# A GRU over 128 steps on one Trainium2 core: x loaded once into a ring of four tiles, and half of each crossing copied by ScalarE

## The chip, the cores and the metric

The kernel runs on one core of a Trainium2 chip. The core has a matrix engine (PE in the profile; PEld is its loading of weights, which overlaps with its products), a vector engine (DVE), a scalar engine (ACT), a general engine (POOL), a sync engine (SP) that here only issues DMAs, and 16 DMA engines. The engines run side by side, each through its own list of instructions in the order written, and they wait for each other by semaphores. The metric is the time of the whole program on the device in microseconds (us); lower is better. A change is called faster or slower here if it is more than 0.5%, about 6 us, away.

## The reference

64 sequences of 128 steps and 512 features go through a gated recurrent unit (GRU) with 512 hidden values, everything in float32. After every fourth step, except the last of all, the state also goes through a product with Wp and a tanh before the next step uses it. The output is x plus the states.

```python
def step(h, inp):
    x_t, prop = inp                          # prop: (t+1) % 4 == 0 and t < 127
    comb = jnp.concatenate([x_t, h], axis=-1)
    z = jax.nn.sigmoid(comb @ Wz + bz)
    r = jax.nn.sigmoid(comb @ Wr + br)
    comb2 = jnp.concatenate([x_t, r * h], axis=-1)
    h_cand = jnp.tanh(comb2 @ Wh + bh)
    h_new = (1.0 - z) * h + z * h_cand
    h_next = jnp.where(prop, jnp.tanh(h_new @ Wp + bp), h_new)
    return (h_next, h_new)                   # scan over T = 128; out = x + all h_new
```

## The kernel before, in words

**Two kinds of work.** The products with the state, h @ W, depend on the step before and form the recurrent chain. The products with x don't, and are made ahead of it as filler: PE runs them while the chain is on the other engines. The 128 steps are 32 groups of four. From group 2 on, two groups (a "duo", 15 of them) are handled together by a scheme of the Strassen and Winograd kind that saves multiplications: a duo has seven `Batch` objects, each of seven sub-products, and each sub-product is a few units of eight matmul instructions in the trace (L695, tiles `x` in PSUM). ACT and DVE bring the sub-products out of PSUM (L725 to L739) into four SBUF tiles `mb`, POOL adds them up there (L303, `mb<-mb,mb`), and the four results of a group are its crossings.

**A crossing.** `send` (L783) takes one result from its `mb` tile to the tile `gx` of a pair of steps. The result is four blocks of 64 partitions by 384 floats: block (h, d) lies on the partitions of half h and belongs on those of half d. All four go by DMA, issued by SP (L789). There are 124 crossings. A step reads its `gx` tile in its gate sums (L1142 and others) and as the start values of its candidate (L987).

**The step.** A step of the chain has seven blocks of 16 matmuls for the gates R and Z (L275; left operands `ht`, results in `bank_A`, `bank_B`, `bank_C`, `bank_E`), two sigmoids on ACT for each half of the batch (L1011), and two candidate products of 32 matmuls (`wc`), each with a tanh on ACT (L1230). From the new state, DVE makes the left operands of the next step: it transposes (L271), ACT copies one piece into PSUM (`first_copy`, L961), and DVE takes sums and differences of the pieces (L968 to L970). The block `bank_E<-wrz` (S1) needs L969, which needs L961. Every fourth step has two more products of 32 (`wp`) and two more tanhs (L1261). The last four steps are computed plainly, with the weights of h unsummed: since the summing overwrote part of Wr and Wz, four pieces of these, 256 KB each, are loaded again (tiles `raw`, L1032).

**What sets the order.** All of it is a list written at build time by a planner in Python. It keeps its own estimates: `clock` (PE's time by fixed costs), `pool_free` and `sync_free`. `fill(n)` puts up to n units of filler at one of the places of a step (`PLACES` and, for steps 0 to 3, `HEAD`). It takes a unit only if its operands are there by the estimates, and it takes a sub-product that writes a new `mb` tile only if the tile's former results have all been sent (`room`, set by `over`). `flush` puts the ACT or DVE evictions behind a sub-product, `drip` issues up to two DMAs per place, a crossing whose sum is done by the estimate or else another DMA, and `have_sums` forces the DMAs of a crossing that a step needs at once. Since the estimates decide which unit stands where, another estimate moves units.

**x.** x is loaded twice. Once into `xr`, a ring of two group tiles in which POOL adds the states to x (L303, `xr<-xr,h`) and from which the result is stored (L1073); and once into `xs` (two tiles, L129), from which DVE makes the transposed x for the filler (`join_x`, L344). At the end the `xs` tiles take the weights `raw`.

Of the kernel before, what the change touches and what calls it, by code (L numbers as in the profile page):

```python
# [9 lines left out]
F32 = mybir.dt.float32  # L10
# [8 lines left out]
def kernel(  # L19
# [14 lines left out]
    nc = tc.nc  # L34
# [17 lines left out]
    const = ctx.enter_context(tc.tile_pool(name="const", bufs=1))  # L52
    one = ctx.enter_context(tc.tile_pool(name="one", bufs=1))
    two = ctx.enter_context(tc.tile_pool(name="two", bufs=2))
    ps_c = ctx.enter_context(tc.tile_pool(name="ps_c", bufs=1, space=PSUM))
    ctx.enter_context(tc.manual_schedule())

# [85 lines left out]
            )  # L143

    both_queues = (nc.sync, nc.scalar)
    xr, xs = {}, {}
# [21 lines left out]
    def landing(name):  # L168
        did.add(name)
        lands[name] = max(sync_free, clock) + 3500  # L170

    def load_xs(g, later=None):
        if g < GROUPS:
            xs[g] = one.tile([P, Q4, S, J], F32, tag=f"xs{g % 2}", name=f"xs_{g}")
            load_x(xs[g], g * Q4, Q4, later)
            if later is None:
                did.add(("xs", g))
            else:
                last = later.pop()
                later.append(lambda: (last(), landing(("xs", g))))  # L180

    new_xr(0)
    x_rows = one.tile([P, Q4, S, J], F32, tag="xs0", name="x_rows")[:B].rearrange(
        "b t h u -> b (t h u)"
    )
    for t in range(2):
        both_queues[t].dma_start(out=x_rows[:, ts(t, D)], in_=x[:, t, :])
    for k0, k1 in ((0, 1), (1, 2), (2, K)):
# [17 lines left out]
    def later_loads():  # L206
        load_w(wrz[:, :, R], Wr[D:])
        load_w(wrz[:, :, Z], Wz[D:])
        load_step(3)
        new_xr(1)  # L210
        load_x(xr[1], Q4, Q4)
        load_w(wc, Wh[D:])
        load_x(xr[0], 0, 2)
        load_xs(2)
        load_w(wp, Wp)
        for q in range(NQ):
            nc.sync.dma_start(
                out=bias_p[part(q)],
                in_=bp.rearrange("(o j) -> o j", o=1)[:, ts(q, J)].broadcast_to([V, J]),
            )  # L220
# [87 lines left out]
            nc.gpsimd.tensor_sub(o, a, b)  # L308
            Gp.busy(o)

    crossing, plain_dmas = [], []

    def issue(run):
        nonlocal sync_free
        run()
        sync_free = max(sync_free, clock) + 690

    def cross():
        ready, run, then = crossing.pop(0)
        issue(run)  # L320
        then()

    def drip(n):
        for _ in range(n):
            if sync_free > clock + 1400:
                return
            if crossing and crossing[0][0] <= clock + 300:
                cross()
            elif plain_dmas:
                issue(plain_dmas.pop(0))  # L330
            else:
                return

# [448 lines left out]

    def send(q, n, g, i):  # L783
        new_gx(q)
        parts = [(h, d) for h in range(S) for d in range(2)]
        for k, (h, d) in enumerate(parts):

            def run(h=h, d=d):
                nc.sync.dma_start(  # L789
                    out=gx[q][ts(d, 2 * V), h, n].rearrange("p b g u -> p (b g u)"),  # L790
                    in_=M[g, i][ts(h, 2 * V), d].rearrange("p b g u -> p (b g u)"),
                )

            def then(k=k):
                if k == len(parts) - 1:
                    sent.add((q, n))
                    over(g, i, sync_free + 2700)

            crossing.append((pool_free, run, then))

    todo = []
    steps_done = -1
# [18 lines left out]
    def join_next():  # L821
        for n, (g, i, after) in enumerate(joins):
            if all(a in did for a in after) and (
                g is None or g < FIRST or ("xs", g) in did and lands.get(("xs", g), 0) <= clock
            ):
# [7 lines left out]
                if i == Q4 - 1 and g >= FIRST:  # L833
                    load_xs(g + 2, plain_dmas)
                if i == Q4 - 1 and g == GROUPS - 1:
                    load_raw()
                poll()
                return True
        return False
# [140 lines left out]

    def have_sums(t):
        while t >= Q4 and not all((t // 2, n) in sent for n in range(C)):
            cross()

    def seed_h(t, lane, h):
        have_sums(t)
# [35 lines left out]
            )  # L1022

    hT = ht.rearrange("p n v -> p (n v)")
    raw_late = []

    def load_raw():
        for k in range(2):
            raw_late.append(one.tile([P, 2, H], F32, tag=f"xs{k}", name=f"raw_{k}"))
            for i in (R, Z):  # L1030
                plain_dmas.append(
                    lambda k=k, i=i: nc.sync.dma_start(  # L1032
                        out=raw_late[k][:, i],
                        in_=gates_in[i][D:].rearrange("(p k) n -> p k n", k=K)[:, k],
                    )
                )

    def gate_product(t, lane, i):
        for k in range(K):
# [29 lines left out]
    def store(g, n):  # L1069
        for h in range(S):  # L1070
            for q in range(NQ):
                plain_dmas.append(
                    lambda h=h, q=q: nc.sync.dma_start(  # L1073
                        out=out[ts(h, V), g * Q4 : g * Q4 + n, ts(q, J)],
                        in_=xr[g][part(q), :n, h, :],
                    )
                )

    def behind(t, h_new):
        nonlocal steps_done  # L1080
        g, j = divmod(t, Q4)
        steps_done = t
        unsaved.append((t, h_new))
        poll()
        if t == T - 2:
            save()
            store(g, Q4 - 1)
            while crossing or plain_dmas:
                cross() if crossing else issue(plain_dmas.pop(0))
        elif j == 0 and g > 0:  # L1090
            store(g - 1, Q4)
        if j == 1 and g >= 1 and g + 1 < GROUPS:
            load_x(lambda: new_xr(g + 1), (g + 1) * Q4, Q4, plain_dmas)
            last = plain_dmas.pop()
            plain_dmas.append(lambda: (last(), did.add(("xr", g + 1))))

    unsaved = []

    def save():
        while unsaved:  # L1100
            t, h_new = unsaved.pop()
            g, j = divmod(t, Q4)
            while g >= FIRST and ("xr", g) not in did:
                issue(plain_dmas.pop(0))
            o = xr[g][:, j].rearrange("p h (e k) -> p h e k", k=K)
            Gp.tensor_add(o, o, h_new.rearrange("p h (k e) -> p h e k", k=K))

    def step(t, h_old, v_1):
# [27 lines left out]
        else:  # L1136
            have_sums(t)
            fill(next(places), eager)
            flush(at_act, 300)
            first_copy()  # L1140
            block(u_ps, A11, raw(0, 0), start=True)
            nc.vector.tensor_add(row[0][:, :J], u_ps, rz_in(t, 0, 0))  # L1142
# [1 line left out]
            save()  # L1144
            fill(next(places), eager)
            flush(at_act, 300)
            block(row[0][:, :J], A12, raw(1, 0))
            block(e_ps, S1, raw(0, 1), start=True)
            flush(at_dve, 0, 1 if t > 3 else 9) or join_next()
# [5 lines left out]
            flush(at_dve, 900, 1 if t > 3 else 9) or join_next()  # L1155
            fill(next(places), eager)
            flush(at_act, 300)
            block(u_ps, S3, summed(3))
            nc.vector.tensor_add(  # L1159
                row[1][:, : 2 * J].rearrange("p (n j) -> p n j", n=2),  # L1160
# [123 lines left out]

    def late_step(t, gate_r, gate_z):
        flush(at_act, 300)
        flush(at_dve, 300)
# [86 lines left out]
    )  # L1374
    for d in range(DUOS):
        add_duo(d)

    for _ in range(2):
        join_next()
    h, v_1 = h_init, None  # L1380
    for t in range(T):
        if t == 1:
            load_xs(3, plain_dmas)
        h, v_1 = step(t, h, v_1)


# [37 lines left out]
```

## Time and profile before

| | |
|---|---|
| time, median of 3 runs | 1266.87 us (1265.43, 1266.87, 1271.63) |
| profiled execution | 1270.18 us; from its first to its last instruction 1268.3 us |
| granted TensorE clock in it | 0.996 |
| busy share of the span | PE 97%, PEld 89%, DVE 71%, ACT 45%, POOL 72% |
| bytes moved by DMA | 112.43 MB, 106.68 MB of them on the queue of SP's and ACT's DMAs |

In the views, a line such as "L695 PE MATMUL x<-sums_w,s ... x8" is a group of 8 instructions of program line 695 that write the tile `x` and read `sums_w` and `s`. In the timeline, the first number is the start in the span, the second the time to the end of the group, and in brackets behind it stands how long the engine idled before it and what ended that ("<-issue": nothing that the profile shows). In the list of waits, the three numbers are us in total, how often, and the longest. The groups overlap, because the engines are pipelined: the time that a group really costs its engine is the distance to the start of the next one.

### The profile page before, as it was taken

Reading aid. Unit: us, or ns where it says so; the run is one execution under the profiler, and the core shown is the slowest. Engines: PE = TensorE matmul, PEld = TensorE weight load, DVE = VectorE, ACT = ScalarE, POOL = GpSimd, SP = SyncE. Lnnn points to the kernel's source line nnn. Section 1 sums busy time; section 2 is a strip of 40 time slices with the busy share of each in tenths; the row PEclk is TensorE's granted clock in tenths of the full one; section 3 lists DMA queues with packets and bytes.
Section 4 is the critical chain, followed back from the end, with each engine's and each line's share of the span. In section 5 each row is a group of like instructions: output and inputs, shape, how many; then the busy total and the mean of one; then the engine's idle time right before and its main releaser. Section 6 shows DMA issues by size and latency. Waiting matters only on the chain.

```text
span 1268.3 us, 85362 instructions
## 1 busy us (share of the span) xinstructions
PE 1233.8 (97%) x37576; PEld 1131.0 (89%) x37576; DVE 900.8 (71%) x2964; ACT 565.1 (45%) x1838; POOL 916.6 (72%) x1045
## 2 busy tenths in 40 slices
PE   7899999999999999999999999999999999999997
PEld 6798999999998999989899999988889999999887
DVE  5656777777776777777777777777777777777665
ACT  1344444444444444444444444444444444444443
POOL 1796787876868778687786868778677786868751
PEclk9999999999999999999999999999999999999999
DMA  7323333333343332333324343332333324333322
GB/s 243 87 51 79 89 92 86 83 92 87 74 102 84 85 90 74 92 96 83 83 71 101 82 102 82 90 89 72 91 82 83 97 73 99 85 90 93 86 61 62
DMA packets 153090, 112.43 MB, mean 89 GB/s; under 512 B 20836, under 2 KB 148976, under 8 KB 152720
## 3 DMA queue, kind: packets, MB, share of 16 engines
q1 hardware_dynamic: 152288, 106.68, 33.2%
q8 instruction: 295, 4.83, 1.7%
q14 instruction: 75, 0.61, 0.2%
q0 software_dynamic: 256, 0.14, 0.0%
q10 hardware_dynamic: 176, 0.16, 0.0%
HBM read 41.36 MB, written 16.78 MB: 46 GB/s over the span
## 4 chain that ended last, share of the span: by engine, by line
PE 95%; issue 2%; DVE 1%; ACT 1%; POOL 1%; DMA 0%; DVEq 0%; POOLq 0%; ACTq 0%
PE x L695 39%; PE bank_B L275 20%; PE bank_C L275 15%; PE bank_A L275 13%; PE bank_E L275 5%; PE x L275 2%; DMA stage<-in_L_cond_bh_dram 0%; POOL wx L308 0%; ACT bank_A L1011 0%; DVE xT L344 0%; DVE h L1234 0%; DVE bank_E L1233 0%; DVE rh L1119 0%; DVE ht L271 0%; POOL stage L191 0%
## 5 line engine op out<-in xcount | busy, mean ns | idle before, releaser
L303 POOL TENSOR_TENSOR mb<-mb,mb 128x768 f32<-128x768 f32 x167 | 304.6, 1832 | 172.5 <-ACT mb L739 82.1
L695 PE MATMUL x<-sums_w,s 128*32 128x192 f32 x2880 | 184.9, 326 | 0.0
L303 POOL TENSOR_TENSOR xr<-xr,h 128x256 f32<-128x256 f32 x127 | 111.3, 876 | 94.8 <-DVE h L1234 94.7
L275 PE MATMUL bank_B<-wrz,ht 128*32 128x128 f32 x4000 | 173.7, 273 | 4.9 <-issue 2.9
L275 PE MATMUL bank_A<-tr,ht 128*32 128x128 f32 x3936 | 168.9, 273 | 1.4 <-issue 0.8
L275 PEld LDWEIGHTS bank_B<-wrz,ht 128*32 128x32 f32 x4000 | 133.0, 110 | 13.4 <-issue 8.8
L275 PE MATMUL bank_B<-wc,rhT 128*32 128x128 f32 x4096 | 142.1, 274 | 2.9 <-DVE rhT L271 0.5
L275 PE MATMUL bank_C<-wc,rhT 128*32 128x128 f32 x4096 | 141.2, 273 | 0.0
L275 PEld LDWEIGHTS bank_A<-tr,ht 128*32 128x32 f32 x3936 | 129.5, 110 | 8.4 <-DVE bank_B L1153 4.2
L275 PEld LDWEIGHTS bank_B<-wc,rhT 128*32 128x32 f32 x4096 | 112.8, 109 | 24.2 <-ACT bank_A L1011 16.0
L695 PE MATMUL x<-sums_w,o 128*32 128x192 f32 x1920 | 124.9, 326 | 1.0 <-issue 1.0
L275 PEld LDWEIGHTS bank_C<-wc,rhT 128*32 128x32 f32 x4096 | 119.8, 110 | 0.5 <-ACT bank_C L1125 0.2
L695 PEld LDWEIGHTS x<-sums_w,s 128*32 128x32 f32 x2880 | 111.3, 110 | 4.9
L1159 DVE TENSOR_TENSOR bank_C<-bank_A,gx 128x256 f32<-128x256 f32 x123 | 53.2, 433 | 82.1 <-PE bank_A L275 82.1
L1011 ACT ACTIVATE bank_A<-bank_B 128x128 f32<-128x128 f32 x123 | 32.2, 262 | 154.6 <-DVE bank_C L1159 151.2
L1119 DVE TENSOR_TENSOR rh<-bank_A,h 128x128 f32<-128x128 f32 x192 | 56.1, 292 | 52.7 <-ACT bank_A L1011 46.2
L725 ACT COPY x<-x 128x384 f32<-128x384 f32 x108 | 50.3, 465 | 86.9 <-PE x L695 86.9
L303 POOL TENSOR_TENSOR mb<-mb 128x768 f32<-128x768 f32 x47 | 86.2, 1834 | 2.5
L731 ACT COPY u<-x 128x384 f32<-128x384 f32 x108 | 51.8, 479 | 78.1 <-PE x L695 78.1
L739 ACT COPY mb<-x 128x384 f32<-128x384 f32 x108 | 52.1, 482 | 77.1 <-PE x L695 73.9
L271 DVE STREAM_TRANSPOSE rhT<-rh 128x128 f32<-128x128 f32 x256 | 79.8, 312 | 9.0
L275 PE MATMUL bank_E<-wrz,ht 128*32 128x128 f32 x1968 | 85.0, 274 | 0.2 <-issue 0.2
(884 smaller groups left out, 3085.6 us busy)
## 6 DMA issues: line engine op xcount, KB each, us to landing
gx<-mb SPq DMA_DIRECT2D x496, 96.0 KB, 2.5
xr<-in_x_dram SPq DMA_DIRECT2D x248, 64.0 KB, 2.8
out_dram<-xr SPq DMA_DIRECT2D x248, 64.0 KB, 2.6
xs<-in_x_dram SPq DMA_DIRECT2D x240, 64.0 KB, 2.9
wx<-in_L_cond_Wz_dram SPq DMA_DIRECT2D x2, 512.0 KB, 6.2
wx<-in_L_cond_Wh_dram SPq DMA_DIRECT2D x2, 512.0 KB, 8.0
wrz<-in_L_cond_Wr_dram SPq DMA_DIRECT2D x2, 512.0 KB, 9.3
wrz<-in_L_cond_Wz_dram SPq DMA_DIRECT2D x2, 512.0 KB, 10.8
```

The source lines that it names most:

```text
L271: nc.vector.transpose(out=dst, in_=src)
L275: nc.tensor.matmul(region[part(q)], lhsT=left, rhs=rhs(q), start=start, stop=True, skip_group_check=True,)
L303: nc.gpsimd.tensor_add(o, a, b)
L695: nc.tensor.matmul(v[part(2 * h + c)], lhsT=left[:, ts(h, V)], rhs=right[:, c::2], start=j in (1, 5) and m == 0 and n == 0, stop=True, ski ...
L725: nc.scalar.copy(self.a, self.u)
L731: nc.scalar.copy(self.u_sb, self.u)
L739: nc.scalar.copy(self.block(1, 0), runs(self.u))
L1011: nc.scalar.activation(gate_out(dst), gate_in(lane, i), AF.Sigmoid)
L1119: nc.vector.tensor_mul(rh[:, h], r_ps[:, h], h_old[:, h])
L1159: nc.vector.tensor_add(row[1][:, : 2 * J].rearrange("p (n j) -> p n j", n=2), bcast(u_ps), G[t][:, 1, :, :2].rearrange("p n g u -> p n (g ...
```

## The change

x is loaded once, into a ring of four tiles `xr`, which serves both the transposes and the output. The tile of group g+3 takes the place of the tile of group g-1; its load is queued behind that group's store, and the planner holds it back until it reckons the store to be done. Of each crossing, the two blocks with h = d are copied by ACT (`staying`, placed by `stay` at three places of a step, after `flush(at_act)`, at most one at each; two in a late step), and the two others go by DMA as before. A tile `mb` counts as free 1000 ns after the copy by the planner's clock, and as before 2700 ns after the last DMA is issued. `have_sums` forces copies as well as DMAs. The weights `raw` now go into `wx`, the weights of x, after the last batch has read it.

```diff
-            xr[g] = two.tile([P, Q4, S, J], F32, tag="xr", name=f"xr_{g}")
+            xr[g] = ring.tile([P, Q4, S, J], F32, tag="xr", name=f"xr_{g}")
...
-    def load_xs(g, later=None):
...
+    def load_group(g):
+        def when():
+            return stored.get(g - 4, 0)
+
+        held_back = []
+        load_x(lambda: new_xr(g), g * Q4, Q4, held_back)
+        last = held_back.pop()
+        held_back.append(lambda: (last(), landing(("x", g))))
+        for run in held_back:
+            plain_dmas.append((when, run))
...
+    def stay(late=200, most=1):
+        while most and staying and staying[0][0] <= clock + late:
+            staying.pop(0)[1]()
+            most -= 1
...
-        src = xr[g] if g < FIRST else xs[g]
+        src = xr[g]
...
-        parts = [(h, d) for h in range(S) for d in range(2)]
-        for k, (h, d) in enumerate(parts):
-
-            def run(h=h, d=d):
-                nc.sync.dma_start(
-                    out=gx[q][ts(d, 2 * V), h, n].rearrange("p b g u -> p (b g u)"),
-                    in_=M[g, i][ts(h, 2 * V), d].rearrange("p b g u -> p (b g u)"),
-                )
...
-                    over(g, i, sync_free + 2700)
+        for h in range(S):
+
+            def run(h=h):
+                nc.sync.dma_start(out=to(h, 1 - h), in_=of(h, 1 - h))
+
+            crossing.append((ready, run, lambda: one_done(sync_free + 2700)))
+            staying.append(
+                (ready, lambda h=h: (nc.scalar.copy(to(h, h), of(h, h)), one_done(clock + 1000)))
+            )
...
         while t >= Q4 and not all((t // 2, n) in sent for n in range(C)):
-            cross()
+            if staying and (not crossing or staying[0][0] <= crossing[0][0]):
+                staying.pop(0)[1]()
+            else:
+                cross()
...
-    raw_late = []
+    raw_late = [wx[:, k, :2] for k in range(2)]
...
             fill(next(places), eager)
             flush(at_act, 300)
+            stay()
             first_copy()
...
+    task("raw", load_raw, ("b", DUOS - 1, 6))
```

On PE, the order differs from step 6 on for a few steps. Before, the candidate products of step 5 (`wc`) and the blocks A11, A12 and S1 of step 6 stand without filler between them:

```order
L275 MATMUL bank_B<-wc,rhT_1818 32x128 x16
L275 MATMUL bank_C<-wc,rhT_1818 32x128 x16
L275 MATMUL bank_A<-wrz,ht 32x128 x8
L275 MATMUL bank_B<-wrz,ht 32x128 x8
L275 MATMUL bank_E<-wrz,ht 32x128 x8
L275 MATMUL bank_A<-tr_86,ht 32x128 x8
L695 MATMUL x_101<-wx,o_2_1428 32x192 x4
```

Of the change, at the same place (its line 279 is line 275 before, 704 is 695):

```order
L279 MATMUL bank_B<-wc,rhT_1803 32x128 x16
L279 MATMUL bank_C<-wc,rhT_1803 32x128 x16
L704 MATMUL x_104<-wx,o_2_1421 32x192 x4
L704 MATMUL x_104<-sums_w,o_2_1421 32x192 x4
L704 MATMUL x_103<-sums_w,s_2_1424 32x192 x8
L279 MATMUL bank_A<-wrz,ht 32x128 x8
L704 MATMUL x_105<-wx,s_2_1424 32x192 x4
L704 MATMUL x_105<-sums_w,s_2_1424 32x192 x4
L704 MATMUL x_102<-sums_w,xT_973 32x192 x4
L279 MATMUL bank_B<-wrz,ht 32x128 x8
L279 MATMUL bank_E<-wrz,ht 32x128 x8
L279 MATMUL bank_A<-tr_89,ht 32x128 x8
```

Four units of filler now stand ahead of A11 and three between A11 and A12 (a unit is x4 here, and eight instructions in the trace); at step 7 it is alike. After step 9 or so, PE's order is the same as before up to the last steps' names.

On ACT, the copies stand between the other work. Before, around `first_copy` (L961) and the gates (L1011) of step 15:

```order
L731 COPY u_4_3919<-x_100 128x384
L733 COPY mb_4_3929<-x_101 128x4x3x32
L961 COPY bank_E<-ht 128x128
L739 COPY mb_4_3929<-x_100 128x4x3x32
L1011 ACTIVATE bank_A<-bank_B 128x128
```

Of the change (L815 is the new copy, L974 `first_copy`, L1027 the gates):

```order
L740 COPY u_4_3894<-x_103 128x384
L742 COPY mb_4_3904<-x_104 128x4x3x32
L815 COPY gx_3683<-mb_1_3087 64x384
L974 COPY bank_E<-ht 128x128
L815 COPY gx_3683<-mb_3_3691 64x384
L748 COPY mb_4_3904<-x_103 128x4x3x32
L815 COPY gx_3683<-mb_3_3691 64x384
L1027 ACTIVATE bank_A<-bank_B 128x128
```

A copy has come right ahead of `first_copy`, and two stand between it and the gates. Of the 248 copies, 73 stand right ahead of a `first_copy`; two are forced ahead of a seed of the candidate at the start of steps 4 and 6, and two each stand ahead of the first gate of steps 124 and 125.

On SP, at the end, the weights of the last steps come late. Of the change (L1048 loads them, L811 is a crossing, L1094 a store):

```order
L1094 DMA out_dram<-xr_22982 32x4x128 x8
L811 DMA gx_26280<-mb_2_25942 64x384 x2
L811 DMA gx_26280<-mb_5_26142 64x384 x2
L1048 DMA wx<-in_L_cond_Wr_dram 128x512
L1048 DMA wx<-in_L_cond_Wz_dram 128x512
L1048 DMA wx<-in_L_cond_Wr_dram 128x512
L1048 DMA wx<-in_L_cond_Wz_dram 128x512
L811 DMA gx_26618<-mb_5_26142 64x384 x2
```

They now stand behind the crossings of the last pair of steps but one (`gx_26280`). Before, they stood ahead of the crossings of four pairs of steps; in the trace of before they are issued from 1164 us to 1171.

More of the change, by code (lines that the diff above doesn't have):

```diff
@@ L170, in landing @@
         lands[name] = max(sync_free, clock) + 3500
-    def load_xs(g, later=None):
[L173 to L183, printed above, removed]
+    def load_group(g):
[7 more added lines that the diff above has]
+            plain_dmas.append((when, run))
+    x_rows = ring.tile([P, Q4, S, J], F32, tag="xr", name="x_rows")[:B].rearrange(
         "b t h u -> b (t h u)"
     )
+    new_xr(0)
     for t in range(2):
@@ L328, in drip @@
                 cross()
-            elif plain_dmas:
-                issue(plain_dmas.pop(0))
+            elif plain_dmas and plain_dmas[0][0]() <= clock + 300:
+                issue(plain_dmas.pop(0)[1])
             else:
@@ L823, in join_next @@
             if all(a in did for a in after) and (
-                g is None or g < FIRST or ("xs", g) in did and lands.get(("xs", g), 0) <= clock
+                g is None or g < FIRST or ("x", g) in did and lands.get(("x", g), 0) <= clock
             ):
@@ L1035, in load_raw @@
                     )
-                )
+                    did.add(("raw", k, i))
+                plain_dmas.append((lambda: 0, run))
     def gate_product(t, lane, i):
+        while t and not {("raw", k, i) for k in range(2)} <= did:
+            issue(plain_dmas.pop(0)[1])
         for k in range(K):
@@ L1076, in store @@
                     )
-                )
+                    stored[g] = max(sync_free, clock) + 3000
+                plain_dmas.append((lambda: 0, run))
     def behind(t, h_new):
@@ L1088, in behind @@
             while crossing or plain_dmas:
-                cross() if crossing else issue(plain_dmas.pop(0))
+                cross() if crossing else issue(plain_dmas.pop(0)[1])
         elif j == 0 and g > 0:
             store(g - 1, Q4)
[L1092 to L1095, printed above, removed]
+            if g + 3 < GROUPS:
+                load_group(g + 3)
     unsaved = []
@@ L1102, in save @@
             g, j = divmod(t, Q4)
-            while g >= FIRST and ("xr", g) not in did:
-                issue(plain_dmas.pop(0))
+            assert g <= FIRST or ("x", g) in did
             o = xr[g][:, j].rearrange("p h (e k) -> p h e k", k=K)
@@ L1286, in late_step @@
         flush(at_act, 300)
+        stay(300, 2)
         flush(at_dve, 300)
```

40 lines of the change are left out of this document (23 added, 17 removed).

## The prediction

> **What bounds the kernel now.** I read the page first, its busy shares, the chain and the DMA part, then the windows, the waits, and the timeline where the change moves something.
>
> ```profile
> PE 1233.8 (97%) x37576; PEld 1131.0 (89%) x37576; DVE 900.8 (71%) x2964; ACT 565.1 (45%) x1838; POOL 916.6 (72%) x1045
> PE 95%; issue 2%; DVE 1%; ACT 1%; POOL 1%; DMA 0%; DVEq 0%; POOLq 0%; ACTq 0%
> q1 hardware_dynamic: 152288, 106.68, 33.2%
> q8 instruction: 295, 4.83, 1.7%
> gx<-mb SPq DMA_DIRECT2D x496, 96.0 KB, 2.5
> xs<-in_x_dram SPq DMA_DIRECT2D x240, 64.0 KB, 2.9
> 100.00:1230.00 1130.00, 1116.34 (x34137) 1027.87 (x34128) 819.08 (x2731) 520.24 (x1692) 844.81 (x959) 1.00 0.35 86
> ```
>
> PE is the bound: 95% of the chain of waits is PE, and DMA has 0% of it. In the steady stretch, 100 to 1230 us (the window's columns are busy time of PE, PEld, DVE, ACT, POOL, then clock, DMA share and GB/s), PE is idle for 1130.0 − 1116.3 = 13.7 us in all. The number of matmuls does not change. So whatever the change frees on the DMA side can come back in the time only out of these 13.7 us, and a little at the two ends; a gain of 0.5% (6.3 us, about the spread of the three runs, and what I take as the least that a measurement tells from no change) would need nearly half of them. What ends this idle time is in the list of waits of the same stretch:
>
> ```profile
> PE x L695 <- issue: 4.5, 11, 1.0
> PE bank_B L275 <- issue: 2.9, 6, 1.1
> PE bank_A L275 <- issue: 1.1, 3, 0.6
> PEld bank_B L275 <- ACT bank_A L1011: 15.9, 69, 0.8
> PEld x L695 <- issue: 11.5, 23, 1.3
> PEld bank_B L275 <- issue: 10.9, 33, 1.4
> ```
>
> No line of PE waits for a DMA. Of PE's own idle time, 4.5 + 2.9 + 1.1 = 8.5 us wait for nothing that the profile shows ("issue"), and most of the rest lies at the place of the next part.
>
> **The change part by part.**
>
> *The order at steps 6 and 7: −2.6 us.* The rows of the order show candidate products, A11, A12 and S1 without filler between them. The timeline of before at these places:
>
> ```profile
> 104.94 1.08 PE L275 MATMUL bank_C<-wc,rhT 128*32 128x128 f32 x32
> 106.54 0.64 PE L275 MATMUL bank_A<-wrz,ht 128*32 128x128 f32 x16 [0.52 <-DVE ht L271]
> 107.73 0.65 PE L275 MATMUL bank_B<-wrz,ht 128*32 128x128 f32 x16 [0.54 <-DVE ht L271]
> 108.36 0.64 PE L275 MATMUL bank_E<-wrz,ht 128*32 128x128 f32 x16
> 108.36 0.38 PEld L275 LDWEIGHTS bank_E<-wrz,ht 128*32 128x32 f32 x16 [0.26 <-DVE ht L969]
> 108.82 0.62 PE L275 MATMUL bank_A<-tr,ht 128*32 128x128 f32 x16
> ...
> 117.16 0.64 PE L275 MATMUL bank_A<-wrz,ht 128*32 128x128 f32 x16
> 118.33 0.64 PE L275 MATMUL bank_B<-wrz,ht 128*32 128x128 f32 x16 [0.53 <-DVE ht L271]
> 118.96 0.65 PE L275 MATMUL bank_E<-wrz,ht 128*32 128x128 f32 x16
> ...
> 195.28 0.65 PE L275 MATMUL bank_B<-wrz,ht 128*32 128x128 f32 x16
> 195.72 0.65 PE L275 MATMUL bank_E<-wrz,ht 128*32 128x128 f32 x16
> ```
>
> The last two rows give the undisturbed distance from one block to the next, 195.72 − 195.28 = 0.44 us, so 0.88 for a product of 32. What goes beyond it, start to start, is lost: 106.54 − 104.94 − 0.88 = 0.72; 107.73 − 106.54 − 0.44 = 0.75; 108.36 − 107.73 − 0.44 = 0.19; 118.33 − 117.16 − 0.44 = 0.73; 118.96 − 118.33 − 0.44 = 0.19. The sum is 2.58 us. Is the filler enough for them? A unit of eight, by its rows (below, 609.26 − 608.94), takes 0.32 us. Four units ahead of A11 last 1.3 us and cover the 0.72; with them A11 ends near 107.6, three units carry PE to 108.5, and the operand that A12 waited for was there at 107.7, that of S1 at 108.3. So all three gaps close, and those of step 7 alike. This filler is missing later, but PE's order is the old one again after some steps, so no gap opens where the units stood. Bounds: by PE's own idle time alone, 0.52 + 0.54 + 0.53 = 1.6; by the start to start sum, 2.6. I take 2.6, since a moved unit fills what the start of the next block shows, not only the idle part.
>
> *Less traffic: −0.5 us (0 to −3.2).* Half of the 496 crossing DMAs go, 248 × 96 KB = 24.4 MB, and the 240 loads of `xs`, 15.7 MB: together 38% of the 106.68 MB on that queue. No transfer is waited for by PE. What could still gain is the "issue" time. It is instruction fetch: the instruction queue moved 4.83 MB in 295 packets, 16 KB each, while PE had 2 × 37576 instructions, 255 for a packet, and the stalls stand that many instructions apart or a multiple of it, as this one:
>
> ```profile
> 608.94 0.53 PE L695 MATMUL x<-sums_w,o 128*32 128x192 f32 x8 [0.99 <-issue]
> 609.26 0.37 PE L695 MATMUL x<-sums_w,xT 128*32 128x192 f32 x4
> ...
> 200.00:300.00 100.00, 99.65 (x3052) 92.03 (x3052) 73.84 (x245) 46.64 (x152) 71.07 (x83) 1.00 0.37 91
> 700.00:800.00 100.00, 99.86 (x3093) 92.21 (x3089) 75.04 (x250) 46.28 (x150) 78.72 (x95) 1.00 0.36 90
> 900.00:1000.00 100.00, 97.22 (x2977) 90.19 (x2973) 71.15 (x239) 46.00 (x151) 71.26 (x79) 1.00 0.33 83
> ```
>
> If fetches waited behind data, the stretches with more traffic would stall more. They don't: PE is at 99.65 and 99.86 us where the DMA share is 0.37 and 0.36, and at 97.22 where it is 0.33. So I take next to nothing, and keep as the bound that the 8.5 us shrink with the bytes: 0.38 × 8.5 = 3.2. The Trainium skill (Runtime: NRT & Kernel Launch, Instruction fetch mechanics) says that instructions are streamed in blocks of 256 while the current one executes and that a boundary is "mostly hidden". The blocks agree with the 255 above, the hiding does not: 8.5 us. By that sentence this term would be nothing, and the sum 0.5 us higher.
>
> *The copies on ACT: +0.6 us.* The trace has no copy from SBUF to SBUF of 64 partitions; the nearest row is an eviction of 384 floats:
>
> ```profile
> 194.20 0.48 ACT L733 COPY mb<-x 128x384 f32<-128x384 f32 x1
> 194.57 0.28 ACT L961 COPY bank_E<-ht 128x128 f32<-128x128 f32 x1
> 195.38 0.22 DVE L969 TENSOR_TENSOR ht<-ht,bank_E 128x64 f32<-128x64 f32 x1
> 195.66 0.44 PEld L275 LDWEIGHTS bank_E<-wrz,ht 128*32 128x32 f32 x16
> ```
>
> It lasts 0.48 us, and the next one starts 0.37 after it. So 248 copies occupy ACT for 92 (at 0.37) to 119 us (at 0.48): its share goes from 45% to between 52 and 54%, and ACT as a whole stays far from the bound. What counts is where the copies stand. The tight place is `first_copy` L961: behind it are L969 on DVE and S1, whose weight load starts at 195.66, as soon as L969 ends at 195.60. 73 copies stand right ahead of it. In this step L961 ends at 194.85 and L969 starts at 195.38, a slack of 0.53; a copy takes 0.37 to 0.48 of it. So between 0.16 and 0.05 us are left, and this costs nothing as long as the copy itself doesn't wait. Bound: if it took 0.1 us more than I reckon, once in each of 15 duos, 1.5 us. The forced copies are the other place, two each at the start of steps 4 and 6 and ahead of the first gates of steps 124 and 125. These rows are of the seeds and tanhs of step 4 and of the gates of 124:
>
> ```profile
> 88.49 0.27 ACT L987 COPY bank_B<-gx 128x128 f32<-128x128 f32 x1
> 89.01 0.28 ACT L1261 ACTIVATE h_3p<-bank_C 128x128 f32<-128x128 f32 x1 [0.25 <-PE bank_C L275]
> ...
> 1240.95 0.26 ACT L1007 ACTIVATE bank_A<-x 128x128 f32<-128x128 f32 x1 [0.34 <-PE x L275]
> ```
>
> Two copies are 2 × 0.37 = 0.74 us; ACT idles 0.25 and 0.34 there, so the tanh comes 0.5 late and the gate 0.4. Behind the tanh PE has filler, in step 6 too by the new order; behind the gate PE has other gate products. From nothing to 2 × 0.5 + 2 × 0.4 = 1.8 us, and I take 0.6, a third, for the tail mostly.
>
> *The ring and its loads: 0.* A load waits on SP for its slot's store, which the planner holds it back for. The first transpose of a group stands at least 3.5 us behind the issue of its load by the planner's clock (`landing`), as before with `xs`, and that load landed after 2.9 us (the row of `xs` above). What is queued behind it on SP are crossings, for which PE waits nowhere in the rows above. If that cover were gone, a transpose on DVE and then filler would come late, one landing at most in each group.
>
> *The weights `raw` at the end: 0.*
>
> ```profile
> 1228.16 2.38 SPq L789 DMA_DIRECT2D gx<-mb  x4
> ...
> 1239.80 0.65 PE L275 MATMUL x<-raw,ht 128*32 128x128 f32 x16
> ...
> DMA to landing us min/median/max: 2.9/3.3/4.3
> ```
>
> The crossing ahead of them starts at 1228.16; with two DMAs in place of four it takes 1.2 us, the four loads as long again and a bit, so the last is issued near 1231.5 and lands by 1235.8 at the longest landing of before. PE wants them at 1239.80: 4 us of cover. If the cover is gone, PE waits one to one.
>
> **Sum.** −2.6 − 0.5 + 0.6 = −2.5 us. The profiled execution took 1270.18 (a span of 1268.3 and 1.9 around it), so 1267.7 on its basis. It lay 3.3 us above the median of the runs; against the median of 1266.87 the forecast is 1264.4, with 1261 (all of fetch's 3.2, no cost on ACT) to 1268.6 (gaps closed by 1.6 only, fetch nothing, ACT 1.8 + 1.5) as its own bounds.
>
> **The rivals.**
>
> *Fetch is eased by the lower traffic, faster by over 0.5%.* The Trainium skill (DMA: Bandwidth & Descriptors, Queues, rings and completion order) says that each DMA engine goes round its queues packet by packet, so an instruction block would wait behind data packets, and less data would mean less wait. As a mechanism of this kernel: the weight loads on PEld wait 11.5 + 10.9 + 2.4 + 1.3 = 26.1 us for "issue" (rows of x and bank_B above; bank_A and bank_C below), some of it hidden behind running matmuls. 38% of that is 9.9 us; with the gaps and ACT as above, 1266.87 − 2.6 − 9.9 + 0.6 = 1255.0.
>
> ```profile
> PEld bank_A L275 <- issue: 2.4, 5, 0.9
> PEld bank_C L275 <- issue: 1.3, 4, 0.5
> ```
>
> Between 3.2 and 9.9 the time lies between 1261 and 1255, and from 4.3 on it counts as faster. Against it are the three windows. 18%.
>
> *Nothing to see.* The gaps close, but PE meets the same waits a step later, since filler is only moved; the time is 1266.87 + 0 to 0.6, about 1267. 15%.
>
> *ACT stands still at a copy, slower.* A copy is placed when the planner reckons POOL's sum to be done, 0.2 us ahead even. If POOL is later than reckoned, ACT waits in front of `first_copy`, and DVE, S1 and the whole chain behind it.
>
> ```profile
> L303 POOL TENSOR_TENSOR mb<-mb,mb 128x768 f32<-128x768 f32 x167 | 304.6, 1832 | 172.5 <-ACT mb L739 82.1
> ```
>
> POOL waits 82.1 us for ACT's evictions L739, and copies ahead of these push them; this would feed back. One such wait of half a sum (0.9 us) in each of 15 duos is 13.7 us: 1264.4 + 13.7 = 1278. It decides from 0.6 us per duo on. Against it: POOL is at 72% and waits often, so that its sums are mostly done well before the copy, and a push of 0.4 us per eviction is small against one sum of 1.83. 11%.
>
> *The weights at the end come late*: by 2 to 3 us if SP is held up by the crossings, 1267, no change. 2%.
>
> **How the numbers follow.** The forecast has 54%. Faster by over 0.5% (below 1260.5) comes from the fetch rival alone: 17%, leaving 1% of it on the near side. Slower (above 1273.2): most of the ACT rival, 11% less 1% for its mild end, 10%. The rest, 73%, is no change that can be measured. The predicted time is 1264.4. The range 1257 to 1274 leaves out the far parts of the first and the third rival, some 8% and 9%; the forecast's own is 1261 to 1268.6.
>
> **What would show it.** In the profile after: at steps 6 and 7 no row of PE with idle time for DVE ht L271; the "issue" lines of PE near 8.5 us in the steady stretch as before (under 5.5 speaks for the fetch rival); ACT at 52 to 54%; no new line of ACT waiting for POOL on the `gx` copies worth more than a few us, and S1 still 0.44 after A12; `raw` waited for by nobody. I am wrong if PE's idle time in the steady stretch is not near 13.7 − 1.6 us, or if ACT copies of `gx` show in the chain of waits.

## The result: about 1% less time, over four times the forecast

| | median | range | runs |
|---|---|---|---|
| before | 1270.16 us | 1265.43 to 1274.95 | 6 |
| the change | 1259.53 us | 1256.0 to 1262.02 | 6 |
| ratio | 0.9906 | 95% interval 0.988 to 0.9932 | |

The ratios, here and below, are estimates over all runs of a comparison with their 95% intervals; the quotient of two medians can differ from them by up to 0.002. Beside other runs of before, on the chip of a later comparison, the change had 0.9916 (0.9897 to 0.9935). So it gains 0.8 to 0.9%, 11 to 12 us, where 2.5 us were forecast. The time lies in the range that was given (1257 to 1274), but by the bound of 0.5% it is faster, which had a chance of 17%, and not unchanged. That it lies in the range says little for the reasoning: the range took in a good part of the fetch rival's times, and the median of before came out 3.3 us higher than in the three runs that the forecast started from.

The profiled execution of the change took 1261.79 us, 1260.0 of it from the first to the last instruction. Its page, in the lines that answer to those of before:

```profile
PE 1227.6 (97%) x37576; PEld 1124.0 (89%) x37576; DVE 902.1 (72%) x2964; ACT 685.0 (54%) x2086; POOL 917.3 (73%) x1045
PE 94%; issue 2%; DVE 2%; ACT 1%; POOL 1%; DMA 0%; DVEq 0%; POOLq 0%; ACTq 0%
q1 hardware_dynamic: 97888, 66.54, 20.6%
q8 instruction: 295, 4.83, 1.6%
L815 ACT COPY gx<-mb 64x384 f32<-64x384 f32 x248 | 126.5, 510 | 3.0
gx<-mb SPq DMA_DIRECT2D x248, 96.0 KB, 2.2
100.00:1230.00 1130.00, 1118.64 (x34431) 1029.21 (x34420) 828.70 (x2761) 641.50 (x1952) 853.43 (x966) 1.00 0.21 53
```

PE is the bound as before, ACT is at 54%, and the queue of the data moved 40 MB less. From 100 to 1230 us PE is idle for 11.4 us instead of 13.7, and it did 294 matmuls more in that time, which at its mean of 0.033 us for each are some 9.6 us of work. So most of the gain came out of time that the page counts as busy. The PE order at steps 6 and 7, and the waits for "issue" from 100 to 1230 us:

```profile
106.63 1.08 PE L279 MATMUL bank_C<-wc,rhT 128*32 128x128 f32 x32
108.80 0.65 PE L279 MATMUL bank_A<-wrz,ht 128*32 128x128 f32 x16
110.21 0.65 PE L279 MATMUL bank_B<-wrz,ht 128*32 128x128 f32 x16
110.83 0.65 PE L279 MATMUL bank_E<-wrz,ht 128*32 128x128 f32 x16
...
117.72 0.65 PE L279 MATMUL bank_A<-wrz,ht 128*32 128x128 f32 x16
119.13 0.65 PE L279 MATMUL bank_B<-wrz,ht 128*32 128x128 f32 x16
119.57 0.65 PE L279 MATMUL bank_E<-wrz,ht 128*32 128x128 f32 x16
```

```profile
PEld x L704 <- issue: 7.0, 14, 1.3
PEld bank_B L279 <- issue: 6.4, 24, 0.9
PE x L704 <- issue: 3.4, 7, 1.1
PEld bank_A L279 <- issue: 1.4, 3, 0.5
PEld bank_C L279 <- issue: 1.3, 4, 0.4
PE bank_B L279 <- issue: 1.0, 3, 0.6
PE bank_A L279 <- issue: 0.8, 3, 0.3
```

With four units (1.30 us) and then three (0.98) between them, the blocks of step 6 now follow each other without a loss but one: 108.80 − 106.63 = 2.17 is 0.88 + 1.30, 110.21 − 108.80 = 1.41 is 0.44 + 0.98, and 110.83 − 110.21 = 0.62 has 0.18 left. Those of step 7 have none (0.44 from A12 to S1). So 2.4 of the 2.6 us came. Beyond them, the weight loads of PE wait 16.1 us for "issue" instead of 26.1, and PE itself 3.4 + 1.0 + 0.8 = 5.2 us instead of 8.5, just under the 5.5 that was to speak for the fetch rival.

**What the rest is, in one measure.** After step 9 PE runs the same list in nearly all kernels of this study, so the same matmul can be compared from trace to trace. I took the stretch from the 3800th to the 36600th matmul, and for every four matmuls in a row what they took beyond the mean of the three fastest traces at that place. Places with more than 0.12 us are the stalls. Nearly all of them, 32 to 78 in a trace, end between 1.8 and 4.0 us after a packet on the instruction queue has started, and the middle half of them between 2.4 and 3.0 us after it. The stall of the prediction's quoted row is such a one: an instruction packet starts at 606.22 and takes 1.38 us, and PE goes on at 608.94, 2.72 us after its start. A packet starts every 4.2 us or so, so this alone could be chance in part. The places tell more: in each of the first twelve traces of the table 79 to 87% of the stalls, with 86 to 95% of their time, lie within four matmuls of one and the same grid with a step of 127.1 matmuls, that is 254 instructions or one packet, where chance would put 7%. The 33273rd, 33400th and 33527th matmuls, for example, come late both in before and in back_blocks. With the stalls that follow a packet taken away, the stretch has almost the same length in every kernel but one:

| kernel | MB on the data queue | stretch, us | stalls behind a packet, us | the rest, us |
|---|---|---|---|---|
| before | 106.7 | 1084.9 | 25.4 | 1059.5 |
| order_only | 106.7 | 1078.6 | 19.4 | 1059.1 |
| x_once | 90.9 | 1077.3 | 17.5 | 1059.8 |
| x_once_order | 90.9 | 1082.2 | 22.8 | 1059.4 |
| act_copies | 82.3 | 1073.7 | 12.9 | 1060.8 |
| act_copies_2 | 82.3 | 1078.4 | 18.6 | 1059.8 |
| the change | 66.5 | 1074.7 | 15.1 | 1059.6 |
| after_again | 66.5 | 1070.2 | 10.4 | 1059.8 |
| no_stores | 50.3 | 1076.1 | 15.8 | 1060.3 |
| back_x | 81.8 | 1074.5 | 14.5 | 1060.0 |
| back_blocks | 90.9 | 1081.6 | 21.4 | 1060.2 |
| traffic_back | 106.2 | 1079.3 | 18.3 | 1061.0 |
| copies_twice | 66.5 | 1100.4 | 32.0 | 1068.4 |

The first twelve rows have a correlation of 0.99 between stretch and stalls, with a slope of 0.96 us per us: what differs between these kernels lies in the stalls. With the traffic the stalls rise by 0.16 us per MB, loosely (correlation 0.65). Each row is one execution, and executions of one kernel, here on different chips, differ by 5 us (the two of the change: 15.1 and 10.4), so a row tells what a difference consists of, not how large it is on average. For that there are the ratios of the timed runs below. (The row of copies_twice has other waits among its 32.0 us, since they too can fall behind a packet. By place, only 14 us of its stalls lie on the grid, as in the change with 14 and 10.)

### The profile page after: what moved, and what is told of

Its sections match the earlier page's. It is cut to its first block, busy times and chain, and to the rows that moved or that the text cites. A ratio compares the mean times of both kernels' runs of the same rounds, so it can differ in the third digit from the quotient of the medians.

```text
span 1260.0 us, 84834 instructions
## 1 busy us (share of the span) xinstructions
PE 1227.6 (97%) x37576; PEld 1124.0 (89%) x37576; DVE 902.1 (72%) x2964; ACT 685.0 (54%) x2086; POOL 917.3 (73%) x1045
## 4 chain that ended last, share of the span: by engine, by line
PE 94%; issue 2%; DVE 2%; ACT 1%; POOL 1%; DMA 0%; DVEq 0%; POOLq 0%; ACTq 0%
PE x L704 39%; PE bank_B L279 20%; PE bank_C L279 15%; PE bank_A L279 13%; PE bank_E L279 5%; PE x L279 2%; ACT bank_A L1027 0%; POOL wx L312 0%; DMA stage<-in_L_cond_bh_dram 0%; DVE xT L353 0%; DVE h L1257 0%; DVE mb L746 0%; DVE bank_E L1256 0%; POOL stage L193 0%; DVE rh L1139 0%
## 5 line engine op out<-in xcount | busy, mean ns | idle before, releaser
L704 PE MATMUL x<-sums_w,s 128*32 128x192 f32 x2880 | 180.7, 326 | 0.0
L279 PE MATMUL bank_B<-wrz,ht 128*32 128x128 f32 x4000 | 171.1, 274 | 4.1 <-issue 2.8
L307 POOL TENSOR_TENSOR xr<-xr,h 128x256 f32<-128x256 f32 x127 | 111.4, 877 | 85.2 <-DMA xr<-in_x_dram 48.7
L279 PE MATMUL bank_A<-tr,ht 128*32 128x128 f32 x3936 | 165.7, 274 | 0.7 <-DVE bank_B L1175 0.5
L279 PEld LDWEIGHTS bank_A<-tr,ht 128*32 128x32 f32 x3936 | 126.5, 110 | 8.4 <-DVE bank_B L1175 4.7
L815 ACT COPY gx<-mb 64x384 f32<-64x384 f32 x248 | 126.5, 510 | 3.0
L704 PEld LDWEIGHTS x<-sums_w,s 128*32 128x32 f32 x2880 | 107.7, 110 | 5.4
L1027 ACT ACTIVATE bank_A<-bank_B 128x128 f32<-128x128 f32 x123 | 32.2, 262 | 103.8 <-DVE bank_C L1182 99.8
L1257 DVE TENSOR_TENSOR h<-bank_E,keep 128x128 f32<-128x128 f32 x254 | 74.1, 292 | 15.2
```

The lines of the kernel that those rows point to most:

```text
L279: nc.tensor.matmul(region[part(q)], lhsT=left, rhs=rhs(q), start=start, stop=True, skip_group_check=True,)
L307: nc.gpsimd.tensor_add(o, a, b)
L704: nc.tensor.matmul(v[part(2 * h + c)], lhsT=left[:, ts(h, V)], rhs=right[:, c::2], start=j in (1, 5) and m == 0 and n == 0, stop=True, ski ...
L815: (ready, lambda h=h: (nc.scalar.copy(to(h, h), of(h, h)), one_done(clock + 1000)))
L1027: nc.scalar.activation(gate_out(dst), gate_in(lane, i), AF.Sigmoid)
L1257: nc.vector.tensor_sub(h_new[:, h], z_h, keep[:, h])
```

## The experiments

Two theories stood against each other. By the first, the gain is PE's order (2.6 us) and something not seen yet; by the second, less traffic on the DMA engines shortens the stalls for instructions. A third question was what the copies on ACT cost.

**order_only.** The kernel before with the change's PE order and nothing else of it:

```diff
-                    over(g, i, sync_free + 2700)
+                    over(g, i, sync_free + (1000 if steps_done < 8 else 2700))
```

> The kernel before; only the planner's time until a tile mb counts as free after its last crossing is 1000 ns instead of 2700 up to step 7. By this alone PE gets the order of the change at steps 6 to 9; no DMA and no copy is changed. Theory order (the closed gaps at steps 6 and 7 are 2.6 us, and nothing else comes of the order): 2.6 us less than before, ratio 0.998. Theory order alone (the whole 12 us of the change come from the order): ratio 0.991. Theory traffic (the rest comes from the removed DMA traffic): 0.998.

Measured: 1261.86 us against 1265.47, ratio 0.9975 (0.9955 to 0.9994), by the ratio 3.2 us less. The order is worth what was reckoned, and it is a quarter of the gain.

**traffic_back.** The change with the removed traffic put back, in a form that nobody waits for:

```diff
                 nc.sync.dma_start(out=to(h, 1 - h), in_=of(h, 1 - h))
+                for _ in range(2 * h):
+                    more_block()
...
         for run in held_back:
-            plain_dmas.append((when, run))
+            plain_dmas.append((when, lambda run=run: (run(), more_x())))
```

> The change with the traffic put back: behind each pair of crossing DMAs two more of 64 partitions of 1536 bytes, and behind each load of x one more of 64 KB, from a tile of weights into a spare piece of DRAM that nobody reads. Nothing waits for them; PE's order is that of the change. Theory traffic: the 9.3 us come back, only 2.6 us less than before, ratio 0.998. Theory order, or any other cause than bytes and DMA counts: ratio stays at 0.991.

Measured: 1267.79 us, ratio 1.0023 (0.9999 to 1.0046). All that the change had gained is gone, the order's share too, though every row of PE and ACT stands where it stood. Late crossings are not the reason: in its list of waits from 100 to 1220 us no line of PE or ACT waits for a DMA, and its rest in the table is 1061.0 us. So traffic on the DMA engines alone, as bytes or as the number of DMAs, which this doesn't keep apart, takes the gain away, and what the change gains beyond the order is put down to the traffic that it removes. The size does not match: put back, the traffic costs 0.011, while its removal gave 0.006 to 0.007. The 39.6 MB here are written to DRAM, where the removed ones went to SBUF; that may be why it is 0.0048 above order_only, which has the same traffic, but no run shows it.

**x_once, x_once_order.** The change without the copies on ACT, all four blocks by DMA; the first with PE's order of before, the second with the new one:

```diff
-        for h in range(S):
+        for h, d in [(h, d) for h in range(S) for d in range(2)]:
...
-                nc.sync.dma_start(out=to(h, 1 - h), in_=of(h, 1 - h))
+                nc.sync.dma_start(out=to(h, d), in_=of(h, d))
...
-            crossing.append((ready, run, lambda: one_done(sync_free + 2700)))
-            staying.append(
-                (ready, lambda h=h: (nc.scalar.copy(to(h, h), of(h, h)), one_done(clock + 1000)))
-            )
+            crossing.append((ready, run, lambda: one_done(sync_free + 2700)))
```

(In the second, 1000 up to step 7 in place of the 2700, as in order_only.)

> The change without the copies on ACT: x loaded once into the ring of four, all four blocks of a crossing by DMA. PE keeps the order of before at steps 6 to 9; 15.7 MB less traffic. Theory traffic (about 9.3 us of the 12 come from 40.1 MB less, in proportion to the bytes, 39% of them here): 3.6 us less, ratio 0.997. Theory order: 1.000.

> The change without the copies on ACT, but with PE's order of the change at steps 6 to 9 (1000 ns for the DMAs up to step 7); two units at step 7 stand one place apart. Beside the order alone (0.9975) it has 15.7 MB less, x loaded once. Theory bytes (the 0.0064 between the order alone and the change go with the 40.1 MB): 0.995. Theory crossings only: 0.9975.

Measured: 1264.84 us, ratio 0.9997 (0.9976 to 1.0018), and 1263.45 us, 0.9978 (0.9956 to 1.0001). With all the crossings still on the DMA engines, loading x once is worth nothing that can be seen: 0.9997 beside 1, and 0.9978 beside the order's 0.9975. A gain in proportion to the bytes (0.997 and 0.995) lies just outside both intervals, but the 0.0064 that it was worked out from is itself uncertain by some 0.003.

**act_copies, act_copies_2.** The kernel before with the copies alone: `send`, `staying`, `stay` and `have_sums` of the change, and everything about x as before. It takes PE's new order with it. The core of it, in the kernel before:

```diff
-            crossing.append((pool_free, run, then))
+            crossing.append((ready, run, lambda: one_done(sync_free + 2700)))
+            staying.append(
+                (ready, lambda h=h: (nc.scalar.copy(to(h, h), of(h, h)), one_done(clock + 1000)))
+            )
...
             flush(at_act, 300)
+            stay()
             first_copy()
```

Timed twice:

> The kernel before with the copies on ACT alone: x loaded twice as before, weights for the end loaded into the tiles of x as before; 24.4 MB less traffic, and PE has the order of the change at steps 6 to 9. Theory traffic: 2.6 for the order and 61% of 9.3 for the bytes, 8.3 us less, ratio 0.9935. Theory order alone: 0.991. If the copies cost ACT's chain more than reckoned, less gain than 2.6.

> The kernel before with the copies on ACT alone once more: x loaded twice, 24.4 MB less, order of the change. Theory bytes: 0.9975 less 61% of 0.0064, 0.9936. Theory crossings only: 0.991, like the change. As measured first: 0.9953.

Measured: 1259.93 us, ratio 0.9953 (0.9932 to 0.9975), and 1260.37 us, 0.9955 (0.9934 to 0.9976). Beside the order alone this is 0.002 less, 2.7 us, and the intervals overlap. The change as a whole is at 0.991, so with the copies made, loading x once is worth another 0.004, 5 us, while without them nothing was seen of it. This difference of 0.004 has an uncertainty near 0.003. A straight line, with 0.0018 for the order and 0.00014 for each MB less, gives 0.9978 and 0.9959 for the two kernels with x loaded once, 0.9947 for the copies and 0.9924 for the change: near the edge of four of the intervals so far, but inside every one. So the runs lean against a gain in proportion to the traffic and don't rule it out.

**back_blocks, back_x.** The change with only one of the two pieces of traffic put back: of traffic_back's edit, the first keeps the call of `more_block`, the second that of `more_x`.

> The change with only the blocks of the crossings put back as traffic, 24.4 MB from a tile of weights into a spare piece of DRAM. Theory bytes: 61% of the 0.0112 by which all of the traffic put back raised the ratio, 0.998. Theory crossings only: 1.002. Theory x only: 0.991.

> The change with only the second load of x put back as traffic, 14.7 MB in pieces of 64 KB from a tile of weights into a spare piece of DRAM. Theory bytes: 39% of 0.0112, 0.9955. Theory crossings only: 0.991. Theory x only: 1.002.

Measured: 1266.09 us, ratio 0.9991 (0.9967 to 1.0015), and 1261.06 us, 0.997 (0.9947 to 0.9993). Each costs, the 24.4 MB 0.008 and the other piece, 15.2 MB by its page, 0.006 against 0.991 (by the medians, 1261.06 beside 1267.27, 0.004); it is not one kind of DMA alone that matters. Together they cost 0.011, which agrees with the sum within the noise.

**no_stores.** The change, with the traffic cut further:

```diff
-                    nc.sync.dma_start(
-                        out=out[ts(h, V), g * Q4 : g * Q4 + n, ts(q, J)],
-                        in_=xr[g][part(q), :n, h, :],
-                    )
+                    if g == GROUPS - 1:
+                        nc.sync.dma_start(
+                            out=out[ts(h, V), g * Q4 : g * Q4 + n, ts(q, J)],
+                            in_=xr[g][part(q), :n, h, :],
+                        )
```

> The change without the stores of the first 31 groups, so their output is not written: 16.3 MB less traffic of 66.5, no row of another engine changed. Theory traffic (fetches of instructions wait behind data): the stalls of PE for issue shrink once more, by 0.2 to 0.35 us per MB as the difference between the change and the change with the traffic put back gives, 3 to 6 us, ratio 0.002 to 0.0045 below the change's. Theory that only the crossings and loads mattered, or that what is left is a floor: the change's ratio.

Measured: 1256.44 us, ratio 0.9923 (0.9893 to 0.9952), beside 0.9916 for the change in the same comparison. No further gain is seen. The two intervals leave room for the smaller part of the gain that was expected (0.002 to 0.0045). The stalls of its one trace, 15.8 us at 50 MB beside 15.1 and 10.4 at 66, say little, since that execution (1263.8 us) was the slowest of its six. The straight line above gives 0.9901, which is inside the interval too.

**after_again.** The change itself, in the comparison of no_stores and copies_twice.

> The change itself once more, on the chip and beside the runs of the other kernels of this batch. Theory sum of the parts (order alone 0.9975, copies with that order 0.9953, x once 0.9997): 0.9953 times 0.9997, 0.995. Theory the first comparison holds: 0.991.

Measured: 1255.38 us, ratio 0.9916 (0.9897 to 0.9935). The first comparison holds, and the parts measured one by one (0.995 together) fall 0.003 to 0.004 short of the whole, by little more than the noise.

**copies_twice.** The change with each copy on ACT made twice:

```diff
-                (ready, lambda h=h: (nc.scalar.copy(to(h, h), of(h, h)), one_done(clock + 1000)))
+                (ready, lambda h=h: (nc.scalar.copy(to(h, h), of(h, h)), nc.scalar.copy(to(h, h), of(h, h)), one_done(clock + 1000)))
```

> The change with each copy on ACT made twice, one right behind the other; 248 copies more, no other row changed. Theory cheap copies: what they cost now is near 0.6 us, and the second one costs as much again, up to 5 us where the slack of 0.53 in one step of eight is already used up by the first; ratio at most 0.004 above the change's. Theory copies on the path (the change would have gained more without them): half a us at each of the 73 places ahead of first_copy and more, over 10 us, ratio 0.008 or more above the change's.

Measured: 1289.83 us, ratio 1.0185 (1.0161 to 1.021), 34 us above the change. This is more than either theory had. The views of who waited, of the change and then of this kernel: for `first_copy` (L974) over the whole span, for the gates (L1027) and the copies from 144 us to 1222 and 1240:

```profile
  DVE ht L982: 2.6, 14
...
PEld bank_B L279 <- ACT bank_A L1027: 18.5, 83, 0.5
PEld bank_B L279 <- ACT gx L815: 0.8, 1, 0.8
```

```profile
  DVE ht L982: 15.8, 44
...
PEld bank_B L279 <- ACT bank_A L1027: 42.3, 89, 1.0
PE bank_B L279 <- ACT bank_A L1027: 17.4, 53, 0.6
PEld bank_B L279 <- ACT gx L815: 2.4, 12, 0.2
```

The weights of the first candidate product (`bank_B`) wait for the sigmoid on ACT for 42 us instead of 18.5, and PE itself for 17.4, where the change has no such row; and behind `first_copy` DVE waits 44 times for 15.8 us instead of 14 times for 2.6. ACT is at 62% only. So the first copy of each block costs next to nothing because it fits into slacks of some tenths of a us ahead of the gates and of `first_copy`, and these are then nearly used up: from 100 to 1230 us the weight loads' wait for the gates had already gone from 15.9 us before to 20.0 with the change, without PE itself waiting. The place ahead of the gates, which the prediction passed over, is the dearer one.

**traffic_more.** The kernel before with 39.6 MB more:

```diff
                 if k == len(parts) - 1:
+                    more_block()
+                    more_block()
...
             load_x(xs[g], g * Q4, Q4, later)
+            if later is not None:
+                later[-8:] = [lambda run=run: (run(), more_x()) for run in later[-8:]]
```

> The kernel before with as much traffic more as the change takes away, in the same form as in the run with the traffic put back: 39 MB into a spare piece of DRAM. PE's order is that of before. Theory traffic: stalls for issue grow by as much as they shrank, 5 to 12 us, ratio 1.004 to 1.009. Theory that the traffic is hidden: 1.000.

Measured: 1373.2 us, ratio 1.0844 (1.0821 to 1.0867). This doesn't answer the question that it was made for: with 480 DMAs more on SP's queue, the crossings themselves came late.

```profile
PE x L718 <- ACT x L748: 59.8, 12, 6.3
...
ACT bank_B L1012 <- DMA gx<-mb: 69.4, 21, 6.1
```

ACT waits 69 us for the `gx` tiles, and PE behind it. What it does show is that the cover of the crossings is gone at this traffic.

## Why the prediction was right or wrong, point by point

- **PE is the bound, and the gain can only come from PE's idle time and stalls.** Right. But the 13.7 us of idle time were no limit, though the gain happened to stay below them: the idle time shrank by 2.3 us only, and the stalls in the stretch measured above add up to 25 us in that execution of before. In its waits for "issue" the weight loads stand for 26.1 us and the matmuls for 8.5, so most of a stall lies inside groups that count as busy. One reading was wrong beside this: of the 5.2 us of idle time that are not "issue", the waits for L271 at steps 6 and 7 are 1.6, not most.
- **The order at steps 6 and 7, −2.6 us.** Right: 2.4 by the rows of the change, 3.2 (0.8 to 5.7) by order_only.
- **Less traffic, −0.5 us (0 to −3.2).** This is the step that failed. From order_only (0.9975) to the change (0.9906 and 0.9916) the traffic is worth 0.006 to 0.007, some 8 us where 0.5 were reckoned, and traffic_back takes more than that back. The mechanism stood in the text as the first rival, with 9.9 us as its upper price and 1255 to 1261 as its time. What failed was the reason against it, the three windows of one execution: in them the DMA share varies by 0.04 only (0.33 to 0.37), while the stalls vary by chance: by 4.7 us over the long stretch between two executions of the change (15.1 and 10.4 us), where the 0.8 MB between the windows shown (83 and 91 GB/s over 100 us), at the 0.16 us per MB of the table, are worth 0.1 us. A comparison inside one trace had no power to exclude it. The bound of 38% of PE's own 8.5 us failed too. 38% of the 26.1 us of the weight loads, 9.9, was close to the 8, and their wait fell by 10.0; since no run confirms a gain in proportion to the bytes, that this share fits so well may be luck.
- **The page of the Trainium skill on arbitration** (DMA: Bandwidth & Descriptors, Queues, rings and completion order), named with that rival, pointed the right way: traffic_back costs 0.011. That an instruction block waits behind data packets is not shown by it, since the data packets' queueing isn't in the trace, and the instruction packets themselves hardly take longer with the traffic (1.18 us on average in the trace of before, 1.13 in that of the change). No_stores and x_once, with less traffic and no gain seen, give it no support.
- **The copies on ACT, +0.6 us.** Right in sum: the rest of the stretch is 1059.6 us for the change, 1059.5 before. A copy is 0.51 us long, a little over the 0.48 of the nearest row, and in the step at 193 us `first_copy` starts 0.54 after it, over the 0.37 to 0.48 reckoned. So the slack of 0.53 at the tight place is just used up: L982 (L969 before) waits for `first_copy` 14 times for 2.6 us in all, of which PE sees next to nothing. ACT's share is 54%, the upper end given. But "far from the bound" was wrong as a judgement, as copies_twice shows.
- **The ring's loads, 0, and the weights at the end, 0.** Right. The weights for the last steps were issued from 1218.8 to 1220.4 and land after 5.1 us at most, and PE takes them from 1228.8 on, 3 us later. The loads of x are less covered than was said: POOL, as it adds the states to x, waits for them 12 times for 48.7 us in all, where it had waited for the states before; PE sees nothing of it.
- **The rival of ACT standing still at a copy.** It did not come: in its view L815 has no line of waiting for POOL, and nobody waits for a copy but one weight load, for 0.8 us.

What stays open: how the traffic makes an instruction packet come so late that PE runs dry, whether the gain goes in proportion to the traffic, and why the traffic put back cost more than its removal gave. Bytes, the number of DMAs and their moments were not told apart.

## What to carry to other kernels

In this kernel, with PE busy at 97%, the stalls for the next block of instructions are a price that data transfers raise, even where PE never waits for a transfer, and another kernel of this kind may pay it too; to see it, compare whole kernels with and without the traffic, several executions each, and not stretches of one trace. An idle engine is no free engine: ACT at 45% took 248 copies for next to nothing at places with a slack of half a us, and the next 248 cost 34 us. And a planner's order can move with a change of a resource's estimate alone, which is worth timing by itself.

## What the runs showed of the hardware that was not expected

- PE's stalls stand some 254 instructions apart, one packet, or a multiple of that, at the same matmuls in different kernels. They end 2.4 to 3.0 us (the middle half) after an instruction packet of 16 KB has started, though the packet itself takes 1.1 to 1.2 us on average, and at full traffic they add up to 18 to 25 us in 1080, at 66.5 MB to 10 to 15.
- Their sum differs by about 5 us between two executions of the same kernel (15.1 and 10.4, 12.9 and 18.6), and with it the length of the stretch: the rest agrees within 2 us over twelve executions of ten kernels.
- 39.6 MB of transfers that PE and ACT never wait for cost 14 us of 1256 when they are put back.
